# Expert weights loaded beside the last routing step, in a kernel of neighbourhood attention, linear attention and a routed expert layer

## The chip, the cores and the metric

The kernel runs on one core of one Trainium2 chip. The metric is the device time of one execution in microseconds. A core has five engines that each work through their own instruction stream in order: PE (TensorE, matmuls; its weight loads are shown apart as PEld), DVE (VectorE), ACT (ScalarE), POOL (GpSimd) and SP (SyncE, which here only issues transfers). Transfers are carried by 16 DMA engines.

## The reference

The input is `x` of shape (2, 56, 56, 256), in float32: 6272 tokens of 256 channels. Two attention layers come first and then the expert layer that the change is about.

```python
x = x + _L0_conv_ref(_gn(x), ...)        # neighbourhood attention, 7 x 7 window, 8 heads
t = _to_tokens(x)
t = t + _L1_attn_ref(_ln_t(t), ...)      # gated linear attention: running sums over the 3136 tokens
t = t + _L1_ffn_ref(_ln_t(t), ...)       # 8 experts, each token goes to its best 2

def _L1_ffn_ref(x, gate_w, gate_b, W1, b1, W2, b2):
    probs = jax.nn.softmax(xf @ gate_w + gate_b, axis=-1)
    top2_vals, top2_idx = jax.lax.top_k(probs, 2)
    cw = zeros.at[arange(N)[:, None], top2_idx].add(top2_vals)
    def step(acc, params):
        w1, bb1, w2, bb2, we = params
        h = gelu(xf @ w1 + bb1)          # 256 -> 512
        y = h @ w2 + bb2                 # 512 -> 256
        return acc + we[:, None] * y, None
```

The kernel computes an expert only for the tokens that chose it.

## The kernel before

**Stages.** The first 600 us or so are the neighbourhood attention. Then `layer1` goes through the tokens in 13 steps of 256 tokens of each of the two images (`NS1` = 13; the last step, number 12, has only 64). Three generators make up a step. `before(s)` normalises and projects the tokens, `attention(s)` does the linear attention and ends with the output projection `p_out` (L1221) and the sum into `x_acc` (L1228), and `route(s)` normalises again into `xs`, computes the gate, ranks the experts, numbers the slots, and scatters each token's row of `xs` to two places of a buffer `xs_d` in device memory (L1340, on POOL). A row is 272 numbers: 256 channels, the token's number, and its weights for the eight experts. `route` ends with `listed(s)`, which writes down which slots of `xs_d` have become full tiles.

**Expert tiles.** A tile is up to 256 slots of one expert. There are 57 of them, numbered k = 0 to 56 in the order in which they are worked: the first 41 are whole tiles, which are sure to be full after given steps, then come seven whole ones and nine halves of 128 slots, mixed. For each tile, `fetch(k)` issues on SP the transfer of its slots (`xg`, L1502, 272 KB) and of its expert's weights (`wj`, L1480, 1154 KB; which expert it is, is known only on the chip). `gather` transposes the slots (`pt_g` on PE, L1553), copies them (`xT_g` on ACT) and has DVE pick the tokens' numbers (`rowk`, L1532) and weights (`cws`, with `own_e`, L1540). `hidden` is the first matrix product and the gelu (`p_h` on PE, L1568; `hT` on ACT, L1575), `results` the second product (`p_y`, L1593), the scaling on DVE (`ye`, L1600; its bias term comes from ACT, L1587) and an indirect transfer from POOL that adds the rows into `out` (L1603). Each tile's adds wait for the previous tile's adds to have landed, and for the stores of the attention's result into `out` (L1244).

**Order.** `together` runs `attention(s)` with `before(s + 1)`, `route(s - 1)` and some expert tiles beside it, a turn of each in proportion. The instructions are then ordered for each engine when the program is built. At s = 13 there is no attention left: `route(12)` runs beside two expert tiles (k = 34 and 35), then `listed(13)` makes the rest of the list.

**Two ways to the weights.** Tiles up to `listed_early()` = 41 load their own weights into one of four buffers `wj` of the pool `fw`. For the tiles from k = 41 on, all eight experts' weights lie in one tile `every_weight` (eight loads of 1154 KB), and `take(k)` has DVE copy the right one into `wj`, in four pieces (L1521). That tile's pool `tw` is opened after `listed(13)`, on the space of the pools `l1` (one buffer a tile) and `l2` (two buffers), which are closed there by `steps.close()`. These hold the tiles of the attention and also those of the routing: `xs`, `xT_f`, `pb`, `rank`, `rowi` and others. A new tile's first write waits for the last use of every tile that lay in its place. `blank()` issues eight small transfers that clear the slots behind the last token of each expert; it comes before the first fetch that needs it.

```python
late = k >= listed_early()
pool = use.rows if late else use.w
...
if listed_early() <= k + 1 < NP:
    take(k + 1)
```

Of the kernel before, what the change touches and what calls it, by code (L numbers as in the profile page):

```python
# [15 lines left out]
F32 = mybir.dt.float32  # L16
I32 = mybir.dt.int32
# [8 lines left out]
NB = 2  # L26
# [53 lines left out]
def listed_early():  # L80
    return sure1(NS1 - 2)
# [731 lines left out]
def layer1(tc, t, out, x1_d, xs_d, ident, load, K, plain, lx, last_rows, lite):  # L813
# [12 lines left out]
    with ExitStack() as whole:  # L826
# [4 lines left out]

        steps = ExitStack()
# [7 lines left out]
        def either(shape, tag):  # L840

            n = taken_from[tag] = taken_from.get(tag, -1) + 1
            pool = use.late if use.late is not None and n % 2 else p1
            return pool.tile(shape, F32, tag=tag, name=tag)

        use = SimpleNamespace(ahead=2, asked=0, late=None)
# [42 lines left out]
        def inverse_root(x, T, n, k=""):  # L889
            y = p2.tile([P, n], F32, tag=f"root{k}{n}", name="root")[:T]  # L890
            a = p2.tile([P, n], F32, tag=f"root_a{k}{n}", name="root_a")[:T]
            nc.vector.tensor_single_scalar(
                a.bitcast(I32), x.bitcast(I32), 1, ALU.logical_shift_right
            )
            nc.vector.tensor_scalar(  # L895
                y.bitcast(I32), a.bitcast(I32), -1.0, float(0x5F3759DF), ALU.mult, ALU.add
            )
            for _ in range(3):
                nc.vector.tensor_mul(a, y, y)
                nc.vector.scalar_tensor_tensor(a, a, -0.5, x, ALU.mult, ALU.mult)  # L900
                nc.vector.scalar_tensor_tensor(y, a, 1.5, y, ALU.add, ALU.mult)
                yield
            return y

        def norm(s, x, at, k):
            W, T, nj = size(s)
            nt = NB * nj
            st = p2.tile([P, NB, NJ, 6], F32, tag=f"st{k}", name="st")
            mv = p2.tile([P, NB * NJ, 2], F32, tag=f"mv{k}", name="mv")
            for i in range(nt):  # L910
                b, j = divmod(i, nj)
                nc.vector.bn_stats(st[:T, b, j, :], x[:T, b, j, :])
                nc.vector.bn_aggr(mv[:T, i, :], st[:T, b, j, :])
                if i % 2:
                    yield
            ve = p2.tile([P, NB * NJ], F32, tag=f"ve{k}", name="ve")
            nc.vector.tensor_scalar_add(ve[:T, :nt], mv[:T, :nt, 1], LN_EPS)
            rs = at_once(inverse_root(ve[:T, :nt], T, nt, k))
            nm = p2.tile([P, NB * NJ], F32, tag=f"nm{k}", name="nm")
            nc.vector.scalar_tensor_tensor(  # L920
                nm[:T, :nt], mv[:T, :nt, 0], -1.0, rs, ALU.mult, ALU.mult
            )
            yield
            for i in range(nt):
                b, j = divmod(i, nj)
                nc.scalar.activation(  # L926
                    at(i), x[:T, b, j, :], AF.Identity, bias=nm[:T, i : i + 1], scale=rs[:, i : i + 1]
                )
                if i % 2:
                    yield  # L930

        def turned(s, at, tag):
            W, T, nj = size(s)
            nt = NB * nj
            xT = p1.tile([P, NG, NB, B1], F32, tag=tag, name=tag)
            for g in range(NG):
                pt = ps_m.tile([P, NB, B1], F32, tag="mm", name="pt_x")
                for i in range(nt):
                    b, j = divmod(i, nj)
                    nc.tensor.transpose(  # L940
                        pt[:, b, j * T : (j + 1) * T], at(i)[:, g * P : (g + 1) * P], ident[:T, :T]
                    )
                nc.scalar.copy(xT[:, g, :, :W], pt[:, :, :W])
                yield
            return xT
# [293 lines left out]
        def route(s):  # L1239
# [29 lines left out]
            lg = p1.tile([P, P], F32, tag="lg", name="lg")  # L1269
# [8 lines left out]
            pb = p2.tile([P, NB * NJ, NE], F32, tag="pb", name="pb")[:T, :nt]  # L1278
            red = p2.tile([P, NB * NJ], F32, tag="red", name="red")[:T, :nt]
# [9 lines left out]
            pairs = p1.tile([P, NG, NB, B1], F32, tag="xT_f", name="pairs").rearrange("p g b n -> p (g b) n")  # L1289
# [9 lines left out]
            rank = p2.tile([P, NB * NJ, NE], F32, tag="rank", name="rank")[:T, :nt]  # L1299
            nc.vector.tensor_reduce(rank, ahead, AX.X, ALU.add)  # L1300
            yield
            taken = p2.tile([P, NB * NJ, NE], F32, tag="taken", name="taken")[:T, :nt]
# [16 lines left out]
            n = p2.tile([P, NB * NJ + 1, NE], F32, tag="n", name="n")  # L1319
# [5 lines left out]
            slot = p2.tile([P, NB * NJ, NE], F32, tag="slot", name="slot")[:T, :nt]  # L1325
            nc.vector.tensor_add(slot, pn[:T, 1, :nt], n[:T, :nt, :])  # L1326
            nc.vector.tensor_tensor(slot, slot, K.c_row[:T, :, 0].unsqueeze(1).to_broadcast(shape), ALU.add)
            rows = p2.tile([P, 2, NB * NJ], F32, tag="rows", name="rows")[:T, :, :nt]
            pick = p1.tile([P, NB * NJ, NE], F32, tag="pick", name="pick")[:T, :nt]
# [3 lines left out]
            rowi = p2.tile([P, 2, NB * NJ], I32, tag="rowi", name="rowi")  # L1333
# [23 lines left out]
        def listed(s):  # L1357
# [4 lines left out]
            new = p2.tile([P, NE], F32, tag="new", name="new")  # L1362
            if last:
                rest = p2.tile([P, NE], F32, tag="rest", name="rest")
                nc.vector.scalar_tensor_tensor(rest, c_prev, -float(SL), n_prev, ALU.mult, ALU.add)
                nc.vector.tensor_single_scalar(new, rest, float(P), ALU.is_gt)
                c = c_prev
            else:
                ci = p1.tile([P, NE], I32, tag="ci", name="ci")
                nc.vector.tensor_copy(ci, n_prev)  # L1370
                nc.vector.tensor_single_scalar(ci, ci, SL.bit_length() - 1, ALU.logical_shift_right)
                c = p2.tile([P, NE], F32, tag="c", name="c")
                nc.vector.tensor_copy(c, ci)
                nc.vector.tensor_sub(new, c, c_prev)
            if hi > lo:
                at = p2.tile([P, NE], F32, tag="at", name="at")
                nc.vector.tensor_tensor_scan(at, K.one8, new, state["at"], ALU.mult, ALU.add)
                state["at"] = at[:, NE - 1 : NE]
                pos = p1.tile(small, F32, tag="pos", name="pos")
                some = p1.tile(small, F32, tag="some", name="some")  # L1380
                first = p1.tile([P, NE], F32, tag="first", name="first")
# [4 lines left out]
                row = p1.tile(small, F32, tag="row", name="row")  # L1386
# [22 lines left out]
        def placed(places_, pos, row, exp, lists):  # L1409
            wide = [P, places_.shape[1], pos.shape[1]]  # L1410
            spare = p1.tile([P, NG, NB, B1], F32, tag="xT_f", name="hits").rearrange("p g b n -> p g (b n)")
            hit, val = (
                spare[:, n, : wide[1] * wide[2]].rearrange("p (k e) -> p k e", e=wide[2]) for n in range(2)
            )
            nc.vector.tensor_tensor(
                hit,
                places_.unsqueeze(2).to_broadcast(wide),
                pos.unsqueeze(1).to_broadcast(wide),
                ALU.is_equal,
            )  # L1420
            add = p1.tile(wide[:2], F32, tag="add", name="add")
            for what, of in zip(lists, (row, exp)):
                nc.vector.tensor_tensor(val, hit, of.unsqueeze(1).to_broadcast(wide), ALU.mult)
                nc.vector.tensor_reduce(add, val, AX.X, ALU.add)
                nc.vector.tensor_add(what, what, add)

        def halved(large, rest, row):

            nh = NP - NW
            over = p1.tile([P, 1], F32, tag="over", name="over")  # L1430
# [7 lines left out]
            second = p1.tile([P, NO - NW], F32, tag="second", name="second")  # L1438
            nc.vector.tensor_scalar(second, K.c_pos[:, 1 : nh - 1 : 2], over, float(P), ALU.is_le, ALU.mult)
            nc.vector.tensor_add(l_half[:, 0, 1 : nh - 1 : 2], l_half[:, 0, 1 : nh - 1 : 2], second)  # L1440
            few = p1.tile([P, NE], F32, tag="few", name="few")
            nc.vector.scalar_tensor_tensor(few, rest, 0.0, large, ALU.is_gt, ALU.subtract)
            at = p1.tile([P, NE], F32, tag="at_half", name="at_half")
# [49 lines left out]
        def fetch(k):  # L1493
            n = parts(k)
            late = k >= listed_early()
# [132 lines left out]
        def experts():  # L1628
            for k in range(NP):
                ask(min(k + use.ahead + 1, len(entry)))  # L1630
                if listed_early() <= k + 1 < NP:
                    take(k + 1)
# [55 lines left out]
        for s in range(NS1 + 1):  # L1688
            others = []
            if s in beside_steps:  # L1690
# [20 lines left out]
            if s == beside_steps[-1]:  # L1711
# [6 lines left out]
                ps_m = steps.enter_context(  # L1718
# [21 lines left out]
        steps.close()  # L1740
        with (
            tc.tile_pool(name="tw", bufs=1, reuse_waits="tile") as tw,
            tc.tile_pool(name="t_ps", bufs=8, space=PSUM, reuse_waits="tile") as ps_t,
            tc.tile_pool(name="tx", bufs=2, reuse_waits="tile") as tx,
            tc.tile_pool(name="tg", bufs=3, reuse_waits="tile") as tg,
        ):
            use.x, use.psum, use.rows, use.ahead = tx, ps_t, tg, 3
            ask(done[0] + use.ahead)
            use.all = tw.tile([P, NE, WJ], F32, name="every_weight")
            for e in range(NE):  # L1750
                weights(use.all[:, e], t["we_parts"][e : e + 1])
            for _ in run:
                pass
# [903 lines left out]
```

## Time and profile before

| | |
|---|---|
| median of three runs | 1374.93 us (1369.16 to 1376.41) |
| the profiled execution | 1428.78 us, of which the span, first to last instruction, is 1427.0 us |
| granted PE clock, mean of the span | 0.938 of full speed |
| busy: PE, PEld, DVE, ACT, POOL | 1268.5, 923.6, 814.2, 583.7, 470.7 us |
| weights: `wj` | 41 loads of 1154 KB |
| weights: `every_weight` | 8 loads of 1154 KB, issued from 1278.56 to 1295.7 us |
| copies from `every_weight`, on DVE | 64, 454 ns in the median |
| adds into `out`, on POOL | 105, of 1592 ns each on average |

The profile is one execution. Its times are microseconds from the start of the span. A busy engine is not thereby the limit: what counts is which wait ended last where PE stood still, and whether another engine's chain ends after PE's. "Idle before" in a row names what released the instruction by the profile's inference. The instruction of POOL or SP that issues a transfer is short; when the transfer has landed is seen from who waits for it.

### The profile page before, as it was taken

How to read it: one execution, taken by the hardware profiler on the slowest of the kernel's cores; microseconds unless marked ns; L12 is line 12 of the kernel's file. 1: busy time of each engine (PE TensorE's matmuls, PEld its weight loads, DVE VectorE, ACT ScalarE, POOL GpSimd, SP SyncE). 2: the span in 40 equal slices, each digit the busy share in tenths (PEclk: the TensorE clock that was granted, in tenths of full speed). 3: DMA queues.
4: the chain of work that ended last, by engine and by line, in shares of the span. 5: the costliest groups of instructions: out<-in, count | busy, mean ns of one | idle time of the engine just before them, and what ended most of it. 6: DMA issues, size and time to landing. Idle time of an engine off the chain costs nothing.

```text
span 1427.0 us, 29974 instructions
## 1 busy us (share of the span) xinstructions
PE 1268.5 (89%) x11566; PEld 923.6 (65%) x11566; DVE 814.2 (57%) x2758; ACT 583.7 (41%) x1053; POOL 470.7 (33%) x514
## 2 busy tenths in 40 slices
PE   2999999899899988788999898989898999886995
PEld 1566667677567764446666676666666677665994
DVE  6445555566666684775656565656565555542540
ACT  1443334444542533235453535344444433532551
POOL 0222222223212333314344334242525154452333
PEclk9999889999996997788999999999999999998998
DMA  8335344333112412206271717161626263689442
GB/s 290 107 107 147 111 147 121 106 110 111 57 45 77 123 60 65 84 20 202 70 217 40 216 37 219 36 206 41 203 52 181 53 189 81 216 230 320 76 70 32
DMA packets 118270, 173.87 MB, mean 122 GB/s; under 512 B 15500, under 2 KB 83596, under 8 KB 118116
## 3 DMA queue, kind: packets, MB, share of 16 engines
q1 hardware_dynamic: 86084, 119.60, 26.5%
q0 software_dynamic: 28864, 47.21, 14.6%
q10 hardware_dynamic: 3168, 5.05, 1.0%
q8 instruction: 93, 1.52, 0.4%
q14 instruction: 61, 0.50, 0.1%
HBM read 123.51 MB, written 48.27 MB: 120 GB/s over the span
## 4 chain that ended last, share of the span: by engine, by line
PE 41%; DVE 12%; ACT 3%; DMA 3%; issue 2%; SPq 1%; POOL 1%; another core or an unknown queue 0%; ACTq 0%; DVEq 0%; POOLq 0%
PE p_y L1593 11%; PE p_h L1568 9%; PE p_qkv L968 7%; PE p_out L1221 3%; PE cx L1203 2%; PE pt_g L1553 1%; PE p_u L990 1%; PE p_sum L1005 1%; SPq L1480 1%; PE cx L1190 1%; ACT xs L926 1%; PE pt_x L940 1%; DMA xg<-xs_d 1%; DVE root L895 1%; DVE am L1152 1%
## 5 line engine op out<-in xcount | busy, mean ns | idle before, releaser
L1603 POOL DMA_INDIRECT out<-ye,rowk x105 | 167.1, 1592 | 369.9 <-DVE ye L1600 162.7
L1593 PE MATMUL p_y<-wj,hT 128*128 128x256 f32 x840 | 211.5, 400 | 6.1 <-DVE am L1152 5.9
L1568 PE MATMUL p_h<-xT_g,wj 128*128 128x256 f32 (+1 forms) x912 | 210.1, 370 | 2.0 <-issue 1.1
L417 ACT ACTIVATE ex<-ex 98x1024 f32<-98x1024 f32 x98 | 103.6, 1057 | 212.7 <-DVE ex L411 208.3
L1593 PEld LDWEIGHTS p_y<-wj,hT 128*128 128x128 f32 x840 | 161.8, 201 | 35.7 <-issue 7.3
L1568 PEld LDWEIGHTS p_h<-xT_g,wj 128*128 128x128 f32 x912 | 155.2, 190 | 25.5 <-issue 6.4
L1575 ACT ACTIVATE hT<-p_h,wj 128x256 f32<-128x256 f32 (+1 forms) x228 | 100.8, 454 | 104.5 <-PE p_h L1568 94.6
L411 DVE TENSOR_TENSOR ex<-sc,bias 98x1024 f32<-98x1024 f32 (+1 forms) x126 | 121.3, 979 | 34.2 <-PE sc L402 30.5
L402 PEld LDWEIGHTS sc<-qb,kc 64*98 64x98 f32 x1568 | 98.1, 172 | 51.4 <-issue 28.1
L425 PE MATMUL po<-vw,ex 98*64 98x33 f32 x3136 | 119.6, 230 | 7.9 <-DMA vw<-v_d 3.5
L402 PE MATMUL sc<-qb,kc 64*98 64x128 f32 x1568 | 122.6, 293 | 3.8 <-DVE slot L1326 1.1
L425 PEld LDWEIGHTS po<-vw,ex 98*64 98x64 f32 x3136 | 107.7, 145 | 25.3 <-issue 6.0
L1340 POOL DMA_INDIRECT xs_d<-xs,rowi x100 | 97.8, 978 | 69.8 <-DVE first L1382 30.6
L1600 DVE SCALAR_TENSOR_TENSOR ye<-p_y,cws,ye 128x256 f32<-128x256 f32 x105 | 50.5, 481 | 120.1 <-PE p_y L1593 108.5
L350 POOL TENSOR_TENSOR xo<-xo,xq 128x256 f32<-128x256 f32 x49 | 36.0, 734 | 249.2 <-DVE xo L344 224.8
L530 PE MATMUL pvv<-L_wvT,xs 128*112 128x256 f32 x224 | 63.5, 424 | 13.8 <-DVE top L522 13.8
L997 DVE TENSOR_TENSOR pd<-p_u,k 128x512 f32<-128x512 f32 (+1 forms) x26 | 17.2, 661 | 97.1 <-PE pt_gate L1273 81.9
L1176 POOL TENSOR_TENSOR zc<-z,blk 128x256 f32<-128x256 f32 x48 | 34.1, 728 | 113.9 <-DVE z L1174 109.7
L1215 ACT COPY cT<-cx 128x256 f32<-128x256 f32 (+1 forms) x50 | 18.2, 364 | 123.0 <-PE p_h L1568 57.2
L352 POOL DMA_DIRECT2D x_d<-xo x98 | 56.8, 581 | 16.8 <-POOL xo L350 14.6
L1203 PE MATMUL cx<-am,kp 128*32 128x128 f32 (+1 forms) x800 | 55.9, 301 | 6.7 <-issue 3.7
L1152 DVE TENSOR_TENSOR am<-sc,upto 128x512 f32<-128x512 f32 (+1 forms) x100 | 60.9, 671 | 0.6 <-PE sc L1143 0.5
(262 smaller groups left out, 2198.3 us busy)
## 6 DMA issues: line engine op xcount, KB each, us to landing
wj<-in_we_parts SPq DMA_DIRECT2D x41, 1154.0 KB
vw<-v_d SPq DMA_DIRECT2D x196, 101.1 KB
xg<-xs_d SPq DMA_DIRECT2D x48, 272.0 KB
every_weight<-in_we_parts SPq DMA_DIRECT2D x8, 1154.0 KB
v_d<-values POOLq DMA_DIRECT2D x28, 231.0 KB
xq<-in_x SPq DMA_DIRECT2D x98, 64.0 KB
x_d<-xo POOLq DMA_DIRECT2D x98, 64.0 KB
x_acc<-x_d SPq DMA_DIRECT2D x24, 256.0 KB
```

What stands on the lines that cost most here:

```text
L402: nc.tensor.matmul(at[p][:KN, b, k], lhsT=keys(i, j, k, b, rows, g), rhs=qb[rows, g, :, b, j * QN : (j + 1) * QN], start=True, stop=True,)
L411: nc.vector.tensor_tensor(ex[:KN, of], sc[:KN].rearrange("n p b k h q -> n p b (k h q)"), bias[:KN, g, of].unsqueeze(2).to_broadcast([KN, ...
L417: nc.scalar.activation(ex[:KN], ex[:KN], AF.Exp)
L425: nc.tensor.matmul(po[b * QN : (b + 1) * QN, hh, :], lhsT=ex[:KN, h // 2, b, k, h % 2, :], rhs=vw[:KN, b, k, hh * (HD + 1) : (hh + 1) * (H ...
L968: nc.tensor.matmul(ps[:, :, :W], lhsT=w[:, kk, g * P : (g + 1) * P], rhs=xT[:, kk, :, :W], start=kk == 0, stop=kk == NG - 1,)
L1152: nc.vector.tensor_tensor(am[:T, h, :, :, :T].rearrange("p b g t -> p (b g) t"), sc[:T, :, :, :T].rearrange("p b g t -> p (b g) t"), K.upt ...
L1203: nc.tensor.matmul(cx[hp, g, :T], lhsT=kp[:T, b, g, hp], rhs=am[:T, h, b, g, :T], start=False, stop=True,)
L1340: put = nc.gpsimd.indirect_dma_start(out=xs_d[:, :], out_offset=bass.IndirectOffsetOnAxis(ap=rowi[:T, c, i : i + 1].bitcast(U32), axis=0), ...
L1568: nc.tensor.matmul(ph, lhsT=w1[:, k, f * P : (f + 1) * P], rhs=xT[:, k, :], start=k == 0, stop=k == NG - 1,)
L1575: nc.scalar.activation(hT[:, f, :], ph, AF.Gelu, bias=b1[:, f : f + 1])
L1593: nc.tensor.matmul(py, lhsT=hT[:, f, u * P : (u + 1) * P], rhs=w2[:, f, :], start=f == 0, stop=f == NF - 1,)
L1603: add = nc.gpsimd.indirect_dma_start(out=out[:, :], out_offset=bass.IndirectOffsetOnAxis(ap=rowk[:, u : u + 1].bitcast(U32), axis=0), in_= ...
```

## The change

The tiles of the routing get pools of their own, `r1` and `r2`, which are opened below `l1` and `l2` and stay open to the end. `l1` and `l2` are closed, and `every_weight` is opened and loaded, at the start of the pass s = 13, ahead of `route(12)` and `listed(13)`. Whether a tile is late is no longer read from its number but from whether `every_weight` is there; as 36 tiles have been asked for by then, tiles from k = 36 on fetch only their slots, into a pool `tg` of four buffers (three before). The pool of PSUM tiles and the pools `fx` and `fs` now serve to the end; the pools `t_ps` and `tx` are gone. The lines of the kernel move by two to four, and by up to fifteen at the end of `layer1`.

```diff
+        r1 = whole.enter_context(tc.tile_pool(name="r1", bufs=1, reuse_waits="tile"))
+        r2 = whole.enter_context(tc.tile_pool(name="r2", bufs=2, reuse_waits="tile"))
         steps = ExitStack()
         p1 = steps.enter_context(tc.tile_pool(name="l1", bufs=1, reuse_waits="tile"))
         p2 = steps.enter_context(tc.tile_pool(name="l2", bufs=2, reuse_waits="tile"))
...
-            pool = use.late if use.late is not None and n % 2 else p1
+            pool = use.late if use.late is not None and n % 2 else r1 if tag == "xs" else p1
...
-            st = p2.tile([P, NB, NJ, 6], F32, tag=f"st{k}", name="st")
-            mv = p2.tile([P, NB * NJ, 2], F32, tag=f"mv{k}", name="mv")
+            pool = r2 if k == "f" else p2
+            st = pool.tile([P, NB, NJ, 6], F32, tag=f"st{k}", name="st")
+            mv = pool.tile([P, NB * NJ, 2], F32, tag=f"mv{k}", name="mv")
...
-            xT = p1.tile([P, NG, NB, B1], F32, tag=tag, name=tag)
+            xT = (r1 if tag == "xT_f" else p1).tile([P, NG, NB, B1], F32, tag=tag, name=tag)
...
-            lg = p1.tile([P, P], F32, tag="lg", name="lg")
+            lg = r1.tile([P, P], F32, tag="lg", name="lg")
...
-            pb = p2.tile([P, NB * NJ, NE], F32, tag="pb", name="pb")[:T, :nt]
+            pb = r2.tile([P, NB * NJ, NE], F32, tag="pb", name="pb")[:T, :nt]
...
         def fetch(k):
             n = parts(k)
-            late = k >= listed_early()
+            late = use.all is not None
             pool = use.rows if late else use.w
...
                 ask(min(k + use.ahead + 1, len(entry)))
-                if listed_early() <= k + 1 < NP:
+                if k + 1 < NP and fetched[k + 1][1] is None:
                     take(k + 1)
...
         for s in range(NS1 + 1):
             others = []
+            if s == NS1:
+                steps.close()
+                ask(done[0] + 2)
+                tw, use.rows = (
+                    whole.enter_context(tc.tile_pool(name=n, bufs=k, reuse_waits="tile"))
+                    for n, k in (("tw", 1), ("tg", 4))
+                )
+                use.all = tw.tile([P, NE, WJ], F32, name="every_weight")
+                for e in range(NE):
+                    weights(use.all[:, e], t["we_parts"][e : e + 1])
+                use.ahead = 3
...
-                ps_m = steps.enter_context(
+                ps_m = whole.enter_context(
                     tc.tile_pool(name="l_mm", bufs=8, space=PSUM, reuse_waits="tile")
                 )
...
         listed(NS1)
-        steps.close()
-        with (
-            tc.tile_pool(name="tw", bufs=1, reuse_waits="tile") as tw,
-            tc.tile_pool(name="t_ps", bufs=8, space=PSUM, reuse_waits="tile") as ps_t,
-            tc.tile_pool(name="tx", bufs=2, reuse_waits="tile") as tx,
-            tc.tile_pool(name="tg", bufs=3, reuse_waits="tile") as tg,
-        ):
-            use.x, use.psum, use.rows, use.ahead = tx, ps_t, tg, 3
-            ask(done[0] + use.ahead)
-            use.all = tw.tile([P, NE, WJ], F32, name="every_weight")
-            for e in range(NE):
-                weights(use.all[:, e], t["we_parts"][e : e + 1])
-            for _ in run:
-                pass
+        for _ in run:
+            pass
```

The other tiles of the routing and of the lists (`red`, `pairs`, `rank`, `taken`, `n`, `slot`, `rows`, `pick`, `rowi`, `ci`, `c`, `at`, `pos`, `hits`, `add` and the like) move from `p1` to `r1` and from `p2` to `r2` in the same manner.

## Prediction

> **What bounds the kernel now.** I read the page's slices first (PE 9 of 10 nearly everywhere, a dip to 6 near the end), then TensorE's timeline over the last 200 us. Tiles of the expert list are numbered k = 0 to 56; the 37th place is k = 36. Each PE row is start, length, work, and in brackets the idle time before it and what ended it.
>
> ```profile
> 1234.11 1.94 PE L1221 MATMUL p_out<-L_woT,cT 128*64 128x256 f32 x8
> ...
> 1272.24 3.62 PE L1568 MATMUL p_h<-xT_g,wj 128*128 128x256 f32 x16
> ...
> 1295.28 3.62 PE L1568 MATMUL p_h<-xT_g,wj 128*128 128x256 f32 x16
> 1311.72 1.11 PE L1553 MATMUL pt_g<-ident,xg 128*128 128x128 f32 x4 [12.82 <-DMA xg<-xs_d]
> 1312.63 5.03 PE L1593 MATMUL p_y<-wj,hT 128*128 128x256 f32 x16
> 1317.49 3.62 PE L1568 MATMUL p_h<-xT_g,wj 128*128 128x256 f32 x16
> ```
>
> Attention ends with p_out at 1236.05. From 1272.24, p_h of k = 36, PE runs without a break until it has nothing for 12.82 us: the rows of k = 40 (`xg`) are not there. The chain of waits says why:
>
> ```profile
> 1273.06 5.29 DMA xs_d<-xs,rowi
> 1278.56 0.40 SPq L1480
> ...
> 1296.20 15.48 DMA xg<-xs_d
> ```
>
> The last routing's scatters land, only then SP may issue the eight `every_weight` loads (1278.56 to 1295.7), and k = 40's fetch lies behind 9.45 MB of them. DVE gets its first weight copy at the same moment:
>
> ```profile
> 1311.35 1.20 DVE L1521 COPY wj<-every_weight 128x577 f32 x3 [15.31 <-DMA every_weight<-in_we_parts]
> ```
>
> The windows (length; PE, PEld, DVE, ACT, POOL busy; clock, DMA share, GB/s) show saturated DMA and the clock falling to half:
>
> ```profile
> 1290.00:1295.00 5.00, 5.00 (x27) 4.41 (x26) 0.48 (x1) 2.09 (x5) 3.08 (x2) 1.00 1.04 402
> 1305.00:1310.00 5.00, 0.00 (x0) 0.00 (x0) 0.00 (x0) 0.00 (x0) 0.00 (x0) 0.50 1.09 330
> ```
>
> Last, POOL's scatter-adds into `out`, each tile's waiting for the previous tile's to land:
>
> ```profile
> 1290.62 1.54 POOL L1603 DMA_INDIRECT out<-ye,rowk  x1 [6.44 <-DMA out<-ye,rowk]
> ...
> 1402.05 1.54 POOL L1603 DMA_INDIRECT out<-ye,rowk  x1 [2.93 <-DMA out<-ye,rowk]
> 1403.90 1.54 POOL L1603 DMA_INDIRECT out<-ye,rowk  x1 [0.30 <-issue]
> 1408.53 1.54 POOL L1603 DMA_INDIRECT out<-ye,rowk  x1 [3.09 <-DVE ye L1600]
> 1413.10 1.54 POOL L1603 DMA_INDIRECT out<-ye,rowk  x1 [3.03 <-DMA out<-ye,rowk]
> ```
>
> A whole tile's pair of adds takes 6.5 us (1402.05 to 1408.53), a half tile's 4.6: nine halves and seven wholes from k = 40 on make 87 us. PE needs 7.3 and 3.7 for the same tiles, 84 us. So POOL is a second bound just behind PE in the tail, and while weights flood the engines a pair takes 9.8 us (1280.79 to 1290.62).
>
> [...] SP's `xg` waited for everything ahead on SP's queue (15.48 us for 272 KB), POOL's adds slowed but went on. [...] the windows show 317 to 403 in the flood. [...] p_y at 1312.63 takes 5.03 us for 3.62.
>
> **The change part by part.** PE's and POOL's instruction orders are unchanged in the built program; DVE, ACT and SP differ only near the end.
>
> 1. Pools r1, r2: same tiles, sizes and buffer counts elsewhere; no instruction is added, so 0 of itself. Its effect is on the weights' first wait: in the built program the first `every_weight` load waits for the last p_out, the ACT copy before it, an earlier DVE and POOL operation of attention, and the DMA eight places earlier, and for no scatter. So it starts at 1236.3, not 1278.56.
>
> 2. SP's order: fetch of k = 36 (1222.27 now), eight weight loads, fetches of k = 37 to 40, eight blanks. Five own loads of 1154 KB (k = 36 to 40) go, the first of which waited 18 us for a buffer. Issuing the eight took 17.1 us; again from 1236.3 it ends at 1253.5, and k = 37's fetch goes at 1253.96 today, so SP loses nothing. Its scatters (POOL, eight from 1242.40 to 1252.3) now share the engines; at the flood's pace (6.4 us from an add's end to its landing) they land by 1259 [...]. k = 37 is wanted at 1275.69, k = 40 at 1299.
>
> 3. Length of the flood. Today 1278.56 to 1311.3 is 32.8 us, with six adds in it. In the tail the DMA share is 0.40 on average; over 7.3 us that is 2.9 us for two adds and one 272 KB fetch (0.8 us at 350 GB/s): 1.05 us an add. 32.8 minus 6.3 leaves 26.5 us for the weights. New company from 1236.3 on: five and a half adds (5.8), eight scatters at 0.35 (2.8, from the share of 1240 to 1255 less one wj), two stores (0.4). Sum 35.5: landing at 1271.8. Bounds: 1265 if nothing but the adds hinders, 1282 if the routing's small rows cost twice as much.
>
> 4. The copies. Twenty-one tiles instead of 16 copy weights, 5 x 4 x 0.454 = 9.1 us more on DVE, which is 30% busy there; hidden except the first. k = 36's copies stand in DVE's order behind the add of p_y's second half (1272.44) and a reduction (ends 1273.05). p_h needs two of the four: 1274.0 against 1272.24, +1.8 us. Queued behind on DVE are the half tiles' list and `rowk`, wanted first by k = 41, 30 us later. ACT's new order puts `ye` of k = 37 to 39 ahead of hT of k = 37; that needs cws of k = 39, which DVE reaches about 1283: another 1.5 us. Sum +3.3; bounds 1.8 and 14 (landing at 1282 and the same tail of waits).
>
> 5. What goes: 12.82 idle, 0.5 on pt_g, 1.4 on p_y [...]: 14.7. Net on PE 14.7 - 3.3 = 11.4.
>
> 6. Late next: POOL. Under the flood add pairs of k = 33 and 34 start at about 1260.7 and 1270.6 (now 1258.2, 1265.4), the four last scatters at 1274.3, then k = 35 at 1279.3, 36 at 1286, and four pairs of 6.4: k = 40 at 1311.6. PE has k = 40's first half ready at 1323.5 - 11.4 = 1312.1. The two meet; with 1312.5 for the start, 87 to 89 us of adds and the 13.9 us from the last pair to the end (1413.1 to 1427.0) the span is 1413 to 1415. I take 1415: 12 us less.
>
> The cover for part 3 is PE's work of k = 33 to 35 and the last routing, 36 us. If it is short, each us of later landing is a us of idle PE at k = 36.
>
> **Against the runs.** The profiled execution took 1428.78 (span 1427.0), the runs' median is 1374.93, 54 us less; the profile's clock is 0.83 to 0.88 between 400 and 700 us but 1.00 in most of the end. The 12 us come out of DMA waits at the end, so I subtract them whole: **1363 us**.
>
> **The rivals.** (a) *The flood collides with routing.* For it: at 1245 to 1250 the engines carry 216 GB/s at share 0.57, so small rows are dear. Against: by the estimate of step 3 all eight scatters take 3 us of the engines. Landing at 1282: PE idles 12 us at k = 36, gain 2 to 3 us: 1372. (b) *POOL's adds become the end.* If the pairs of k = 33 to 37 run 8 us later than step 6 has them, k = 40 starts near 1320, the end comes 88 + 13.9 us after, and the gain is 5: 1370. Against: 30 us of drained queue from 1280 on. (c) *The change does not do what it says*: the loads start no earlier, because a tile under `every_weight` still belongs to the last routing. Then DVE's copy for k = 36 stops its queue, and PE, until 1311: 39 us idle at 1272 instead of 14.7: 1400. It decides from a landing later than 1286; slower by over 0.5% from 1293. The built waits speak against it.
>
> **Chances.** Forecast 0.65, (a) 0.17, (b) 0.11, (c) 0.07. A measurement of this kernel can tell about 0.5% (6.9 us) from no change. Of the forecast nearly all, and a little of (a) and (b), is beyond it: faster 0.70, same 0.23, slower 0.07. The forecast's own range is 1358 to 1368; taking in (a) and (b), and below a better flood and a stall longer in runs than in the profile, 1356 to 1373.
>
> **What would show it.** `every_weight` issues from about 1236; DVE's wait for it ends at 1268 to 1277; no idle PE over 5 us after 1272; clock 1.00 there; adds back to back on POOL from 1255 to the end. Wrong if the first weight load starts after 1260, if PE waits over 8 us at k = 36, or if the last p_y moves by 11 us and the end by less than 6.

## The result, and the profile after

The changed kernel took 1359.49 us in the median of five runs (1356.2 to 1366.29), the kernel before 1374.93 us, 15.4 us more; the ratio on record, which is not that of the medians, is 0.9899 with an interval of 0.9863 to 0.9935, or 13.9 us. Timed again beside other runs of the kernel before it was 0.9919 (0.9892 to 0.9946), about 11 us (9.2 between the medians). The forecast was 1363 us.

The two profiled executions differ by 71 us in span (1427.0 and 1355.8), most of it in the first 1240 us, which the change does not touch: there the end of the last p_out came at 1236.05 and at 1175.31. So everything below is told from the **end of the last p_out**, written as +us; from there to the end of the span the kernel before took 190.95 us and the changed one 180.49. Of the three profiled executions of the kernel before, two ran long (1428.78 us here, and 1382.54 in experiment 1, in a slower state that some executions show) and only that of experiment 10, of 1366.83, was like the timed runs, so shares of the gain that are told below from the mean of the three are good to about 2 us.

TensorE's timeline after (start, length, engine, line, work, in brackets the idle time before and what ended it): the last p_out, a short wait and a slow product behind it, p_h of k = 36, p_h of k = 40, and the longer of two late stalls.

```profile
1173.37 1.94 PE L1225 MATMUL p_out<-L_woT,cT 128*64 128x256 f32 x8
1177.80 0.41 PE L1313 MATMUL p_n<-taken,every 128*128 128x32 f32 x2 [2.48 <-DVE taken L1307]
...
1178.26 3.55 PE L1597 MATMUL p_y<-wj,hT 128*128 128x256 f32 x8
...
1209.99 3.69 PE L1572 MATMUL p_h<-xT_g,wj 128*128 128x256 f32 x16 [2.01 <-DVE wj L1525]
...
1240.03 3.62 PE L1572 MATMUL p_h<-xT_g,wj 128*128 128x256 f32 x16
...
1283.67 2.86 PE L1597 MATMUL p_y<-wj,hT 128*128 128x256 f32 x12 [1.76 <-ACT hT L1579]
```

The 12.82 us for `xg` are gone. In their place stand 2.01 us for the first weight copy at k = 36. p_h of k = 40 runs at +64.7; in the kernel before it ran at +81.4 (1317.49). SP's and VectorE's timelines after:

```profile
1175.46 17.70 SPq L1484 DMA_DIRECT2D every_weight<-in_we_parts  x8
1196.17 10.04 SPq L1506 DMA_DIRECT2D xg<-xs_d  x4
```

```profile
1209.38 1.57 DVE L1525 COPY wj<-every_weight 128x577 f32 x4 [0.74 <-DMA xg<-xs_d]
```

The loads start 0.15 us after the last p_out, 42.4 us earlier than before, and their first use starts at +34.1. The releaser in that bracket is a guess of the profile: in a second profile of the same kernel it reads `every_weight<-in_we_parts`, at +32.7. The windows (length; PE, PEld, DVE, ACT, POOL; clock, DMA share, GB/s) show transfers as dense as before (the share is a sum of packet times and can pass 1), now with PE at work beside them and the clock whole:

```profile
1185.00:1190.00 5.00, 5.00 (x27) 4.41 (x26) 1.36 (x8) 3.77 (x9) 3.78 (x5) 1.00 1.04 409
...
1205.00:1210.00 5.00, 2.99 (x15) 2.32 (x13) 3.95 (x26) 0.20 (x1) 0.00 (x0) 1.00 1.12 322
```

Last, POOL's timeline after: the first adds of k = 35, 36 and 40, and of the last whole tile.

```profile
1220.32 1.59 POOL L1607 DMA_INDIRECT out<-ye,rowk  x1 [0.30 <-issue]
1222.21 1.55 POOL L1607 DMA_INDIRECT out<-ye,rowk  x1 [0.30 <-issue]
1229.74 1.54 POOL L1607 DMA_INDIRECT out<-ye,rowk  x1 [5.97 <-DMA out<-ye,rowk]
...
1255.36 1.55 POOL L1607 DMA_INDIRECT out<-ye,rowk  x1 [2.96 <-DMA out<-ye,rowk]
...
1342.07 1.54 POOL L1607 DMA_INDIRECT out<-ye,rowk  x1 [2.83 <-DMA out<-ye,rowk]
```

VectorE's timeline, `ye` of k = 40 and the last `ye` of all:

```profile
1245.63 0.48 DVE L1604 SCALAR_TENSOR_TENSOR ye<-p_y,cws,ye 128x256 f32<-128x256 f32 x1 [2.98 <-PE p_y L1597]
...
1335.68 0.48 DVE L1604 SCALAR_TENSOR_TENSOR ye<-p_y,cws,ye 128x256 f32<-128x256 f32 x1 [1.31 <-ACTq L703]
```

k = 40 is added at +80.05, though VectorE's `ye` for it was there at +70.8. From k = 40 to the last pair at +166.8 POOL hardly waits for anything but its own adds; 13.7 us later the span ends. The last `ye`, made from PE's last product, had been done at +160.85, 13.3 us earlier than before (+174.1), while the end came only 10.5 earlier.

### The profile page after: what moved, and what is told of

It is laid out like the page before. It is cut to its first block, busy times and chain, and to the rows that moved or that the text cites. A ratio compares the mean times of both kernels' runs of the same rounds, so it can differ in the third digit from the quotient of the medians.

```text
span 1355.8 us, 29993 instructions
## 1 busy us (share of the span) xinstructions
PE 1240.0 (91%) x11566; PEld 906.1 (67%) x11566; DVE 808.4 (60%) x2778; ACT 585.8 (43%) x1053; POOL 471.5 (35%) x514
## 5 line engine op out<-in xcount | busy, mean ns | idle before, releaser
L1597 PE MATMUL p_y<-wj,hT 128*128 128x256 f32 x840 | 201.1, 385 | 8.9 <-DVE am L1156 5.9
L1597 PEld LDWEIGHTS p_y<-wj,hT 128*128 128x128 f32 x840 | 153.6, 191 | 36.0 <-issue 7.3
L411 DVE TENSOR_TENSOR ex<-sc,bias 98x1024 f32<-98x1024 f32 (+1 forms) x126 | 121.2, 979 | 34.3 <-PE sc L402 30.9
L916 DVE BATCH_NORM_STATS2 st<-x_acc 128x6 f32<-128x256 f32 (+1 forms) x100 | 38.1, 411 | 51.6 <-DMA x_acc<-x_d 51.2
L1180 POOL TENSOR_TENSOR zc<-z,blk 128x256 f32<-128x256 f32 x48 | 37.8, 885 | 82.5 <-DVE z L1178 78.4
L352 POOL DMA_DIRECT2D x_d<-xo x98 | 56.8, 581 | 16.8 <-POOL xo L350 14.6
L1591 ACT ACTIVATE ye<-wj,cws 128x256 f32<-128x256 f32 x105 | 49.5, 506 | 27.8 <-DVE own_e L1544 17.5
L530 PEld LDWEIGHTS pvv<-L_wvT,xs 128*112 128x112 f32 x224 | 39.2, 189 | 27.2 <-DVE top L522 18.8
```

Source lines behind the costliest of these rows:

```text
L352: nc.gpsimd.dma_start(out=x1_d[b, i * QT : (i + 1) * QT, j * QT : (j + 1) * QT, :], in_=xo[b * QN : (b + 1) * QN, :],)
L411: nc.vector.tensor_tensor(ex[:KN, of], sc[:KN].rearrange("n p b k h q -> n p b (k h q)"), bias[:KN, g, of].unsqueeze(2).to_broadcast([KN, ...
L530: nc.tensor.matmul(ps, lhsT=xs[:, b, k, j * TT : (j + 1) * TT], rhs=wv[:, k, :], start=k == 0, stop=k == NG - 1,)
L1597: nc.tensor.matmul(py, lhsT=hT[:, f, u * P : (u + 1) * P], rhs=w2[:, f, :], start=f == 0, stop=f == NF - 1,)
```

## The experiments

**What was to be told apart.** The theory after the result: the early loads free PE by about 16 us, and POOL's chain of adds, slowed by the flood of weights, takes some 4 of them back; it, not PE, sets the new end. Rivals: PE sets the end; part of the gain is elsewhere; the early start is worth little and it is the five loads left out that pay. Ratios are to the kernel before, run on the same chip; "stretch" is the time from the end of the last p_out to the end of the span.

**1. The kernel before, unchanged.**

> The kernel before, unchanged, for a second profile of it. The two profiles at hand differ by 60.7 us already at the end of the last p_out (1236.05 before, 1175.31 after), ahead of the stretch that the change touches; from there to the end they differ by 10.5 us (190.95 and 180.5). Theory: the 60 us are the first profiled execution's own. Then this profile's last p_out ends near 1185, and from there to the end it takes 189 to 192 us, ratio 1.00. Rival: the routing's own pools speed up the earlier steps too; then the last p_out ends near 1236 again in this profile.

1371.56 us, ratio 0.999 (0.9969 to 1.0011): what the timing gives for no change. The last p_out ended at 1187.58, so the 60 us were the first profiled execution's own and not the pools' doing. Its stretch was 193.22 us, a little over what was expected. PE waits at the same place as in the prediction's profile, and longer:

```profile
1262.56 1.12 PE L1553 MATMUL pt_g<-ident,xg 128*128 128x128 f32 x4 [16.83 <-DMA xg<-xs_d]
```

**2. Only the pools.** The routing's tiles move to `r1` and `r2`, and `fx` serves the tail in place of `tx`; the rest stays as it was, the loads written after `listed(13)`. Against the changed kernel (the block at s = 13, which goes, and smaller parts are left out):

```diff
...
-            late = use.all is not None
+            late = k >= listed_early()
...
         listed(NS1)
+        steps.close()
...
+            use.all = tw.tile([P, NE, WJ], F32, name="every_weight")
+            for e in range(NE):
+                weights(use.all[:, e], t["we_parts"][e : e + 1])
```

> Only the routing's pools r1 and r2 (and fx kept for the tail in place of tx, for space); the loads still stand behind the last routing in the program, and k = 36 to 40 load weights of their own. In the built order the eight loads nevertheless move ahead of the blanks, mixed with the own loads. Theory (in the tail POOL's chain of adds sets the end, and it is late in proportion to how long weights flood the engines): the flood is 5.9 MB or 17 us longer than in the changed kernel, two more pairs of adds take 9.6 us for 6.4; from the last p_out to the end 184 to 188 us, ratio 0.995 to 0.998. Rival (PE alone sets the end): no stall of PE, 178 us, ratio 0.990. Second rival (early loads come from the program's order, not from the pools): as before, 191 us, ratio 1.00.

1367.59 us, ratio 0.9975 (0.9958 to 0.9992); the stretch 186.81, inside the expected 184 to 188. SP's timeline shows that the order is made when the program is built, not by the place in the code: with no scatter left to wait for, two of the eight loads go at +0.15, and the others follow with the tiles' own `wj` among them.

```profile
1172.04 0.93 SPq L1484 DMA_DIRECT2D every_weight<-in_we_parts  x2
1178.54 0.38 SPq L1484 DMA_DIRECT2D wj<-in_we_parts  x1
...
1192.66 0.46 SPq L1484 DMA_DIRECT2D every_weight<-in_we_parts  x1
...
1195.78 15.97 SPq L1484 DMA_DIRECT2D every_weight<-in_we_parts  x5
```

PE still stands 4.47 us at +55.3 for rows that lie behind these loads:

```profile
1227.18 1.11 PE L1557 MATMUL pt_g<-ident,xg 128*128 128x128 f32 x4 [4.47 <-DMA xg<-xs_d]
```

The pools alone are worth 4.6 us of the stretch (191.4, the mean of three profiles of the kernel before, less 186.8), or 3.1 against the 189.89 of experiment 10 alone.

**3. The early loads, but own weights up to k = 40.** The changed kernel with one line as it was.

```diff
-            late = use.all is not None
+            late = k >= listed_early()
```

> The changed kernel, but k = 36 to 40 load their own weights again, behind the eight loads. Theory: wj of k = 36 lands 3.5 us after the eight, so PE waits about 6 us there (2.0 in the changed kernel); the flood is 17 us longer and POOL's chain 6 to 8 us later; from the last p_out to the end 186 to 190, ratio 0.996 to 1.000. Rival (the own loads cost nothing, all of the gain is in the early start): 180 to 182, ratio 0.990 to 0.992.

1366.57 us, ratio 0.9957 (0.9941 to 0.9972); the stretch 184.48, 1.5 us below the range expected. The wait at k = 36, expected at 6 us, is 1.91 us, now for its own load: that part of the expectation was a miss, and k = 40's adds start at +82.4 instead of +80.05. So fetching only slots is worth 4.4 us of the stretch (184.48 less 180.1, the mean of two profiles of the changed kernel); pools and early start without it are worth 6.9 of 11.3 (5.4 of 9.8 against experiment 10 alone). So the early start gains even with the tiles' own loads.

**4. Half the flood.** The changed kernel loads and copies only the first two of each expert's four pieces; the second matrix and the biases of late tiles are left out (the first half stands in their place; the part of the edit at the copies is not shown).

```diff
...
-                    weights(use.all[:, e], t["we_parts"][e : e + 1])
+                    nc.sync.dma_start(
+                        out=use.all[:, e, : WJ // 2].rearrange("p (n c) -> p n c", n=WP // 2),
+                        in_=t["we_parts"][e : e + 1, : WP // 2].rearrange("o n p c -> (o p) n c"),
+                    )
```

> The changed kernel with half of each expert's weights loaded into every_weight (the first half, which the copies use twice): this leaves out the second weight matrix and biases of the late tiles. Theory: the flood is 13 us shorter, add pairs of k = 34 and 35 take 6.4 for 9.5 us, POOL's chain starts its back-to-back run 5 to 6 us earlier, and the wait of 2.0 us at k = 36 stays at about 1 (DVE's order): from the last p_out to the end 174 to 176 us against 180.5, ratio 0.985. Rival (PE sets the end): 179 us, ratio 0.989.

1356.35 us, ratio 0.989 (0.9857 to 0.9922); the stretch 174.14, 6.0 below the changed kernel's mean. TensorE's and POOL's timelines of this kernel, p_h and the first add of k = 40:

```profile
1245.53 3.62 PE L1575 MATMUL p_h<-xT_g,wj 128*128 128x256 f32 x16
```

```profile
1253.35 1.75 POOL L1610 DMA_INDIRECT out<-ye,rowk  x1 [3.47 <-DVE ye L1607]
```

The last p_out ended at 1180.96. So PE reaches k = 40 at +64.6, as with the whole flood (+64.7; +62.8 in experiment 5), but the add starts at +72.4 instead of +80.05 (+78.3 in experiment 5) and waits for `ye`, not for the adds before it. PE's wait at k = 36 is gone, but a slow product (5.41 us for 3.62, at +26) and a longer wait for `taken` ahead of it cost PE about as much, so PE comes no earlier; POOL comes 5.9 to 7.7 us earlier, and the end follows POOL. The ratio alone is the rival's 0.989; what decides is the stretch, where the rival had 179. (By the stretch, 17 us less than before, the ratio would be 0.987, inside the interval.)

**5. The changed kernel again.**

> The changed kernel once more, to size the gain more narrowly. From the end of the last p_out to the end of the span, the kernel before took 190.95 and 193.2 us in two profiles and the changed one 180.5. Theory (all of the gain lies in this stretch): 180 to 181 us again, and a ratio of 0.990 to 0.993. Rival (part of the gain lies elsewhere, since the first comparison gave 13.9 us between medians): a ratio of 0.987 to 0.990, with the same 180 us in the stretch.

1364.36 us, ratio 0.9919 (0.9892 to 0.9946), stretch 179.71. The ratio agrees with the gain in the stretch, 11.3 us between means (9.8 against experiment 10 alone), and the last p_out ends no earlier in the changed kernel (1175.31 and 1182.49) than in experiment 10 (1175.01). So no part of the gain is seen outside the stretch; the interval alone doesn't rule out the rival's 0.990. The first comparison's 13.9 us, which the expectation calls a difference of medians, is that of the ratio.

**6 and 7. Two chains of adds**, in the changed kernel and in the one before. Odd places from k = 37 on are written into a buffer of their own, and a tile waits only for the tile two before it; the adding of the odd tiles is left out.

```diff
-            before_it = added[-1] if added else []
+            before_it = (added[-2] if k >= 37 else added[-1]) if added else []
...
-                    out=out[:, :],
+                    out=apart_d[:, :] if odd else out[:, :],
...
-                    compute_op=ALU.add,
+                    **({} if odd else dict(compute_op=ALU.add)),
```

> The changed kernel, in which every second late tile's rows (odd places from k = 37 on) are written plainly into a buffer of their own instead of being added into out, and each tile's transfer waits only for that of the tile two places before. It leaves out the adding of those tiles. Theory (POOL's chain of adds, not PE, sets the end of the changed kernel): the adds no longer lie behind each other; the last pair starts at about 161 us after the last p_out, right behind PE's last product, instead of 166.8; the late waits of PE for hT, 1.8 and 1.0 us, go, and the stretch to the end takes 173 to 175 us, 6 to 7 less. Rival (PE sets the end and POOL is only even with it): 179 to 181 us, as before the edit.

> The same edit in the kernel before: odd places from k = 37 on are written plainly into a buffer of their own, each tile's transfer waits only for that of the tile two before; the adding of those tiles is left out. There the last pair of adds starts 3 us after the last ye, for the 12.8 us wait of PE at k = 40 let POOL catch up. Theory (in the kernel before PE, stopped by the late rows, sets the end, and POOL adds 3 to 5 us): the stretch from the last p_out to the end falls from 191-193 to 186-189 us, ratio 0.997. With the other run of this edit, the change is then worth 12 to 14 us, what PE gained, instead of 10.5. Rival (POOL's chain takes the same from both): both fall by the same, and the difference between them stays at 10 to 11 us.

In the changed kernel: 1349.48 us, ratio 0.983 (0.9797 to 0.9863), stretch 168.73; one of the six executions took 2385.78 us, for a reason that is not known, and the ratio leaves it out (the median of the other five is 1348.59). In the kernel before: 1368.24 us, ratio 0.996 (0.9938 to 0.9982), stretch 184.76. Both fell further than expected, and the change came to be worth 16 us, not 12 to 14. POOL's waits (who waited for what: total us, times, longest), first those of the changed kernel, then those of the changed kernel with two chains:

```profile
POOL out L1607 <- DMA out<-ye,rowk: 51.8, 16, 6.0
```

```profile
POOL out L1611 <- DVE ye L1607: 34.7, 10, 4.4
POOL apart_d L1611 <- DVE ye L1607: 20.8, 11, 3.8
```

With one chain POOL waits for its own adds, with two it waits for `ye`, that is for PE. (A plain write is also issued in some 0.5 us less than an add, 0.97 to 1.11 us for mostly 1.54 to 1.56, so the edit shortens POOL's own work as well as its waits; the runs don't part the two.) Without the chain the change is worth 16.0 us (184.76 less 168.73), what PE gains; with it about 11 (means of 191.4 and 180.1 us over three and two profiles). The edit takes 6.6 us from the kernel before and 11.4 from the changed one, so the chain gives back 4.8 us (6.2 against experiment 10 alone). With two chains PE still stops at k = 40 in the kernel before, by its timeline; in the changed one it waits 1.82 us at k = 36 and then no more than 0.6:

```profile
1255.76 1.12 PE L1556 MATMUL pt_g<-ident,xg 128*128 128x128 f32 x4 [14.82 <-DMA xg<-xs_d]
```

**8. The loads held back.** The changed kernel, each weight load waiting for the last routing's scatters.

```diff
-                for e in range(NE):
-                    weights(use.all[:, e], t["we_parts"][e : e + 1])
...
-                upto_k = min(upto_k, done[0] + 2)
+                upto_k = min(upto_k, done[0] + (1 if s == NS1 else 2))
...
         listed(NS1)
+        for e in range(NE):
+            waits_for(weights(use.all[:, e], t["we_parts"][e : e + 1]), *puts[NS1 - 1])
```

> The changed kernel, but each of the eight weight loads waits for the scatters of the last routing, as the first one had to in the kernel before (and k = 35 is started after the routing instead of beside it, so that nothing waits in a circle). Nothing is left out. This is the forecast's case of loads that start no earlier. Theory (PE has only k = 33 to 35 and the routing to hide the flood, 36 us, and every us of later landing is a us of idle PE at k = 36): the loads start 40 us or more after the last p_out, land at about 75, PE stands for some 39 us at the first product of k = 36, the stretch takes 212 to 218 us, the run about 1400 us, ratio 1.015 to 1.021. Rival (fetching slots only is what gains, and the early start is worth little): the stretch takes 180 to 193 us, ratio below 1.

1387.42 us in the median of four runs, ratio 1.0105 (1.0061 to 1.015): about 1% slower than before, stretch 202.07. So fetching only slots, without the early start, loses; that rival is out. The direction is the theory's, the size was overrated: without k = 35 beside it the routing scatters 14 us sooner than in the changed kernel (the last four from +25.7 instead of +39.5), so the loads start at +32.3 and the first copy at +61.3, not 75. SP's and TensorE's timelines:

```profile
1210.63 16.57 SPq L1484 DMA_DIRECT2D every_weight<-in_we_parts  x8
```

```profile
1240.20 5.09 PE L1572 MATMUL p_h<-xT_g,wj 128*128 128x256 f32 x16 [28.66 <-DVE wj L1525]
```

The first copy comes 27.2 us later than in the changed kernel and PE idles 26.7 us longer: us for us, as the prediction had it. The end moves by 22: the last `ye` comes 24.6 us later (+185.43), with PE's two late stalls gone, and POOL is less far behind PE, with 16.6 us from the last `ye` to the end for 19.6 in the changed kernel. The product after the idle time takes 5.09 us for 3.62.

**9. Seven buffers for `ye`.** One number of the changed kernel.

```diff
-                    for n, k in (("fs", 8), ("fx", 2), ("fy", 6), ("fw", FW))
+                    for n, k in (("fs", 8), ("fx", 2), ("fy", 7), ("fw", FW))
```

> The changed kernel with seven buffers for the tiles ye instead of six. In the changed kernel the scaled bias that ACT writes into ye waits for the adds that free the buffer (10.1 us in seven waits), hT behind it comes late, and PE loses 1.8 and 1.0 us. Theory (POOL's chain of adds sets the end; PE's late stalls are only its echo): one tile more of room, so the two stalls shrink or go and the last ye comes 1 to 3 us earlier, but the adds start when they did and the stretch from the last p_out to the end stays at 179 to 181 us; ratio 0.990 to 0.993. Rival (PE's late stalls lengthen the run): the stretch falls to 176 to 178 us, ratio 0.987 to 0.990.

1363.78 us, ratio 0.9924 (0.9896 to 0.9952), stretch 179.68. PE's late stalls are gone. VectorE's last `ye` and POOL's last pair of adds (last p_out ended at 1180.02):

```profile
1336.11 0.48 DVE L1604 SCALAR_TENSOR_TENSOR ye<-p_y,cws,ye 128x256 f32<-128x256 f32 x1 [1.31 <-PE p_y L1597]
```

```profile
1346.19 1.54 POOL L1607 DMA_INDIRECT out<-ye,rowk  x1 [2.89 <-DMA out<-ye,rowk]
```

The last `ye` is done at +156.6 instead of +160.85 (+159.9 in experiment 5): PE finishes 3.3 to 4.3 us sooner, more than was expected, and the last pair starts at +166.2 (+166.8 and +165.8 with six buffers), so the end does not move. This is the plainest proof that PE does not set it. It also shows what the stall at 1283.67 was. ACT's timeline of the changed kernel, just ahead of it:

```profile
1282.75 0.51 ACT L1591 ACTIVATE ye<-wj,cws 128x256 f32<-128x256 f32 x1 [3.14 <-DMA out<-ye,rowk]
```

ACT's `ye` waits for the add that frees its buffer, hT stands behind it in ACT's order, p_y behind hT. With seven buffers ACT has no such wait, and the stall is not there. POOL's chain pushes back on PE through the buffers.

**10. The kernel before, a third profile.**

> The kernel before once more, for a look at its end in another execution. In one profile PE reached the first product of k = 36 at 36.2 us after the last p_out, with a 3.2 us wait for xT_f on the way, and then stood 12.8 us for the rows of k = 40; in another it was there at 32.5 us without that wait and stood 16.8 us. Theory (the restart at k = 40 is set by the weights' landing and not by PE, so a stall on the way is absorbed there): k = 40 restarts at 74 to 76 us again, and the start of k = 36 and the idle time there add up to 48 to 50 us; the stretch takes 190 to 194 us. Rival: the restart moves with PE's arrival.

1366.83 us in the one run, stretch 189.89. TensorE's timeline, p_h of k = 36 and the restart (last p_out ended at 1175.01):

```profile
1207.52 3.62 PE L1568 MATMUL p_h<-xT_g,wj 128*128 128x256 f32 x16
...
1249.89 1.11 PE L1553 MATMUL pt_g<-ident,xg 128*128 128x128 f32 x4 [16.71 <-DMA xg<-xs_d]
```

k = 36 starts at +32.5, the restart comes at +74.9. In the prediction's profile these were +36.2 and +75.7, and in experiment 1 +32.5 and +75.0: the start of k = 36 and the idle time add up to 49.0, 49.2 and 49.3 us. The landing of the transfers, of k = 40's rows behind the weights, sets the restart; where PE loses time ahead of it doesn't matter. The 12.82 us of the one profile were what was left after a stall of 3.18 us, `p_gate<-xT_f,gw`, that the others don't have.

## Why the prediction was right

The forecast held, in its sign, its mechanism (an early start of the loads, the wait for rows gone, POOL's adds just behind PE) and its size (12 us; 13.9 and 11.1 by the ratios, 11.3 in the stretch). Two of its terms were off, PE's gain by 5 us or more and POOL's start by 2.7 to 4.5; the first made PE too slow and the second POOL too fast. That the size came out so near is in part luck: the first error had no effect, since POOL sets the end, and of the second, part was made good by two smaller ones (see the sum).

- **Step 1, the start.** Right: the first load was forecast 0.3 us after the last p_out and came after 0.15. Experiments 2 and 8 show both sides of it: with only the pools free, the loads move ahead by themselves; tied to the scatters again, all is lost and more.
- **Step 2, SP.** Right: PE never waits for `xg` after the change. The 17.1 us of issue became 17.7, and the fetches went from +20.9 to +30.9, the first three us later than forecast, ahead of need.
- **Step 3, the flood.** Forecast landing 35.5 us after the start, +35.75; the first copy starts at +34.1 and +32.7. A sum of bytes and shares of company is good to 2 to 3 us here.
- **Step 4, the first copy.** Forecast 1.8 us at k = 36, from DVE's order alone, measured 2.01 and 2.33; DVE itself stood 0.74 and 1.06 us just ahead of the first copy. The 1.5 us for ACT's new order behind it did not come: from there to k = 40 no wait of PE in the first profile is over 0.31 us.
- **Step 5, PE's gain.** Forecast 11.4 net, measured 15.6 to 18.6 at p_h of k = 40 (+64.7 and +62.8 after; +81.4, +80.3 and +80.4 in the three profiles of the kernel before), 16.7 between the first two profiles. The term that failed is the 12.82 us: it should have been about 16.8, since 3.7 us of PE's lateness, 3.18 of them one stall that only this profile has, had been absorbed in that wait (experiment 10); the 1.5 us of step 4 are the rest. A wait's length in one profile is a difference of two arrivals; the gain was to be taken from the arrival that goes.
- **Step 6, POOL.** The order of waits was right, "the two meet" was not: k = 40's adds were forecast at +75.6 (1311.6) and came at +80.05 and +78.3. k = 33 and 34 were right within 1.3 us, k = 35 began 1.8 and 0.9 late, and from k = 36 on the period of 6.4 held; what was mis-sized most is the pair of k = 35, 6.7 us forecast, 9.4 and 8.1 measured. Its second add is issued by 1223.76 and lands only at 1229.74, in windows in which the DMA share is 0.33 to 0.55 (1.04 to 1.12 in the flood), so the transfers had drained, as the case against rival (b) had it, and the pair was slow all the same. Experiment 4 shows that it goes with the flood's length: with half of it the wait behind this pair is 3.1 us at most, and k = 40's adds wait for `ye`. There the same four scatters and eight blanks go ahead of the pair, closer than in the changed kernel, so neither holds it up by itself. What does is open. The sign "adds back to back from 1255 on", +19, came only from k = 36 on, +54.
- **The sum.** From 1312.5 for k = 40, 88.6 us of adds and 13.9 us the stretch was to be 179; it took 180.5 and 179.7 (+80.05, 86.7 and 13.7). So of the 3.6 us by which k = 40's adds were late in the first profile, 2.1 were made good by adds and an end that were shorter than forecast. PE's larger gain did not matter, since the chain sets the end.
- **Rates and clock.** Windows of the flood, of 5 us each, show 322 to 409 GB/s (1180 to 1210), where the profile before had 317 to 403 (1280 to 1310). Where the wait was long, slow products followed: 5.09 us for 3.62 after 28.66 idle in experiment 8, and in the profile before 5.03 for 3.62 after 12.82, at a granted clock of 0.50 from 1305 to 1315. For shorter waits the runs are mixed: in the changed kernel 2.48 us of waiting and a few small products were followed by 3.55 us for eight products of p_y (1178.26; clock 0.81 from 1180 to 1185), in the profile before nearly the same wait (2.50 us) by 1.97 (clock 1.00 from 1240 to 1245). From 1185 to 1260 the changed kernel's clock is 1.00.
- **The rivals.** (a), a collision with the routing, did not come: PE waits 2 us at k = 36. (b), POOL's adds as the end, is half true: the pairs run 2.7 to 4.5 us later, not 8, but PE comes at least 5 us earlier than the forecast had it, so POOL is the end, by the 11.4 us that experiment 6 takes off. (c) was shown in experiment 8 to be slower, by 1%; its price of 1400 us was too high there, as the scatters landed sooner.

No version that does all the work was faster than the changed kernel: experiment 9 is even with it, and the two shorter ones, 4 and 6, leave work out. What they point to is the chain of adds; a way to shorten it that leaves no adds out was not tried.

## What to carry to other kernels

When a big load waits at the boundary of two stages, ask which tile's last use holds its space; giving the tiles that outlive the stage a pool of their own is what let the load start 42 us earlier: in experiment 2, with the loads still written at their old place, the first of them went just as early. Before pricing a wait, add the time of arrival to it, and see in a second profile which of the two is steady. When PE is freed, look for the next chain in the same stretch, and test it by giving the stalled engine room (one more buffer): if the stalls go and the end stays, the chain that frees the buffers is the bound.

## What the runs showed of the hardware

- An indirect add of 128 rows mostly takes POOL 1.54 us to issue (up to 1.83), a plain indirect write of as many rows 0.97 to 1.11 us, by POOL's timelines of the changed kernel and of experiment 6, from which these lines are:

```profile
1244.68 1.83 POOL L1611 DMA_INDIRECT out<-ye,rowk  x1 [0.30 <-issue]
1248.45 1.06 POOL L1611 DMA_INDIRECT apart_d<-ye,rowk  x1 [1.94 <-DVE ye L1607]
...
1255.71 1.56 POOL L1611 DMA_INDIRECT out<-ye,rowk  x1 [0.31 <-issue]
```

- From the end of an add's issue to the release of the next by its landing it takes 2.8 to 3.2 us for most pairs of the quiet end (single ones are longer), 6.2 to 7.7 us while weights flood the engines (kernel before, experiments 1 and 10), and 4.5 to 6.0 us for one pair some 10 us after the flood (changed kernel, experiments 5, 6 and 9).
